# A fused Mamba-2 and MoE-LoRA layer on one core: places of the first products, the base weight sums, the convolution's Silu and the accumulator loads

## The chip, the cores and the metric

The kernel runs on one core of one Trainium2 chip. The metric is the device time of one execution in microseconds (us): from the first to the last work of the program on the core. All data are fp32.

The core's engines run beside one another, each its own instructions in a fixed order: TensorE (PE in the profile) multiplies matrices, VectorE (DVE) and ScalarE (ACT) work on elements, GpSimd (POOL) works on elements too, and SyncE (SP) issues the transfers between DRAM and the on-chip memories. An instruction that is not ready holds up everything behind it on its engine.

## The reference, cut to what matters

One layer over a sequence of 2048 positions with 1024 channels. Two branches share one layer norm:

```python
xn = layernorm(x)                                   # x: (1, 2048, 1024)
# branch 1: Mamba-2 block
gate, hbc, dt = split(xn @ in_proj_w.T)             # 4096, 4096 + 2*1024, 64 channels
xBC  = silu(conv_bias + 4-tap causal conv(hbc))     # per channel
xs, B, C = split(xBC)                               # 64 heads x 64; 8 groups x 128; 8 x 128
dt   = softplus(dt + dt_bias);  dA = exp(dt * A);  A = -exp(A_log)
state = state * dA + (dt * xs) outer B              # for each position, 64 heads
y    = state . C + D * xs
y    = rms_norm(y, groups of 512) * norm_weight * silu(gate)
mamba = y @ out_proj_w.T                            # 4096 -> 1024
# branch 2: linear layer with a mixture of LoRA experts
w    = softmax(top2(xn @ W_router.T))               # 8 experts
ffn  = xn @ W_base.T + b_base + 2 * sum_e w_e * ((xn @ A_e.T) @ B_e.T)   # rank 16
out  = x + mamba + ffn
```

The recurrence is computed by chunks of 128 positions: inside a chunk as a masked product of matrices, from chunk to chunk by a state that each head carries along.

## The kernel before, in words

**Tiles.** The sequence is taken in two parts (`s`, 1024 positions each). A part has two halves of 512, and a half has four chunks of 128. A "block" in the main loop is one group of eight heads in one half of one part: 32 blocks, numbered `b` from 0, four chunks each.

**Projections.** All large products use a recursive scheme with seven products of half-size matrices in place of eight. In the input projections and in the base layer a *pair* of weight tiles (two times 128 output channels) is one such unit: `pair` (from L450) runs seven products for it, and each is four matmuls of 128x128 by 512 positions. Its operands on the weight side come from `left_operands` (from L413): the quarters `a11`, `a12`, `a22` and the sums `s1` to `s4`. With `fresh` set, the sums are made by GpSimd from the quarters and stored to DRAM, to be loaded when the same weights come again; without it they are loaded from there (`kept`). Results leave PSUM through `stored` (from L517): an addition on VectorE or a copy on ScalarE into a tile `ev` (four buffers), for the gate also a Silu on ScalarE, then a store to DRAM. The very first pair is made of four plain products (`plain_pair`, from L497), since its operands arrive piece by piece; a plain product's result is scaled by the layer norm's reciprocal deviation when it leaves PSUM.

`in_pairs` (from L551) gives the order of the pairs. For each part it goes through the eight groups, with three pairs for x, B and C and two for the gate each; then come the base layer's four pairs for part 1, and for part 0. A pair's operands are requested one pair ahead (`ahead`). `stream` is the running list of all products.

**The start.** The layer norm of part 0 is computed in four pieces of 256 positions (`ln_first`, from L194). Each piece passes through steps: mean (`ps_mean`), subtraction and squares, variance (`ps_var`, then Sqrt on ScalarE and a reciprocal on VectorE), scaling. `small_first` (from L884) multiplies the scaled channels by the narrow weights (step sizes, router, LoRA) for two chunks per call, into `ps_sm`. L894 to L912 write out the order of these steps and of the first pair's products on TensorE. `small` (from L297) turns the results into step sizes (softplus), decays (`at`, and `ex` by an Exp on ScalarE, L330), running decays and router weights. For part 1 this is done within blocks 2 to 13, by pieces 0 to 3.

**The convolution.** `load_raw` (L608) brings a block's raw channels, and `conv` (from L624) works on them in steps, one per tile of 128 channels: the first tap by ScalarE (Identity, L635), three more taps by VectorE (L641), and after every second tile a Silu on ScalarE (L647). The main loop runs these steps for the next block during chunks 1 and 2 of the present one, four steps each.

**The scan.** `scan_a` (from L673) prepares a chunk one chunk ahead, in three steps: the scan of decays `es` on VectorE (L682); the product `ps_cb` and its masked form, with `bt` on ScalarE (L694); and the transposition `ps_xt` on TensorE, after which ScalarE writes `xdt` in eight instructions, one per head, each a copy scaled by that head's step size (L707). GpSimd makes `xdd` from it (L83). `scan_b` (from L720) then runs the chunk's products: `ps_y` needs `xdt`, `ps_e` needs the state, `ps_st` needs `xdd` and updates the state. After a block, `norm_squares` and `norm_mean` (L797, `ps_nv`) give the group norm; `ps_nv`, `ps_xt` and `ps_cb` use the same PSUM bank in turn (`aux`).

**Sums for the output weights.** `out_sums` (from L829) makes the first-level sums of `out_proj_w` in 16 units `wo_0` to `wo_15`, one per block from block 15 on: four loads in chunk 0 into a tile with one buffer (tag `wo`, pool opened at block 14), GpSimd additions and stores in chunks 1 to 3.

**Output stage.** From L1045 on: four passes (`t`) of seven units (`u`), each with seven products (`w2` weight tiles, seven buffers, loaded in order ahead of use, L1052). Operands are quarters of y (`load_quarter`, L1076) and their differences on VectorE (`level_one`, `level_two` with tiles `t2`). Results are added into four accumulators, which start as quarters of x (`load_acc`, L1149) and receive the base layer and the LoRA product in `finish_acc` (L1159). Work beside the products is put into `side`, a list of steps for each of the unit's seven products.

**What sets the order.** A planner places each instruction on its engine by estimated times, except those that are pinned with `keep_in_program_order`: these keep the order of the program among themselves and against their neighbours on the engine. All TensorE work is pinned, and GpSimd's work for part 1 (`gp`, L81). Before the change neither the Silu of L647 nor the `xdt` of L707 is pinned. SP's transfers stand in one queue in the order in which they are issued; a store in it waits for the instruction that writes its tile, and a load for its buffer.

## Time and profile before

Three runs took 3481.16, 3479.97 and 3479.03 us; the median is 3479.97. One more execution was profiled, and all rows are from it.

| | |
|---|---|
| median of three runs | 3479.97 us (3479.03 to 3481.16) |
| the profiled execution's own time | 3474.15 us |
| its span | 3471.9 us, at a mean granted clock of 0.995 |
| TensorE without work | 57.5 us of the span |
| DMA | 762.44 MB, mean 220 GB/s |
| HBM | 509.30 MB read, 250.61 MB written |

How to read it: times are in us from the start of the span unless they are called ns. PE is TensorE's matmuls and PEld its weight loads, which overlap them; DVE is VectorE, ACT ScalarE, POOL GpSimd, SP SyncE. A row `PE ps_y L79 <- ACT xdt L707: 9.7, 6, 3.1` says that matmuls into `ps_y`, recorded at line 79, waited for ScalarE's writing of `xdt` at line 707: 9.7 us in all, 6 times, 3.1 at the longest. Line 79 is the helper through which all matmuls go, line 83 the one for GpSimd, so the tile's name tells them apart. In a row of a timeline the first number is the start, the second the length of the group, then engine, line, operation, what is written and read, the shape, the count, and in brackets the wait just before with what ended it. A row of a window gives start:end, its length, the busy time and number of instructions of PE, PEld, VectorE, ScalarE and GpSimd, the granted TensorE clock (1.00 is full speed), DMA's mean busy share and GB/s.

### The profile page before, as it was taken

The numbers are of one execution on the slowest core, as the hardware profiler recorded it, in microseconds if no ns is written. First come the engines' busy times: TensorE is split into PE (matmuls) and PEld (weight loads), VectorE is DVE, ScalarE is ACT, GpSimd is POOL, SyncE is SP. The second block draws the span as 40 slices with busy tenths as digits, with TensorE's granted clock in tenths as the row PEclk, the third lists the DMA queues.
The fourth block names the chain that finished last, engine by engine and source line by source line (L and its number), as shares of the span: only waits on it lengthen the run. The fifth ranks groups of instructions, "written<-read, shape, count | busy, mean of one in ns | idle before, by whom it ended". The sixth has DMA issues, their size and how long they took to land. (4 is left out here: it accounts for less than half of the span.)

```text
span 3471.9 us, 37572 instructions
## 1 busy us (share of the span) xinstructions
PE 3414.4 (98%) x12818; PEld 1995.3 (57%) x12818; DVE 2531.1 (73%) x2861; ACT 933.1 (27%) x2160; POOL 845.3 (24%) x571
## 2 busy tenths in 40 slices
PE   8999999999999999999999999999999999999999
PEld 7444544554554544454445454544444588888888
DVE  6647887887887976687878778878775466666665
ACT  2213343333343333333333233333322000000000
POOL 3233333233333211232233332333442000000000
PEclk9999999999999999999999999999999999999999
DMA  6545565666666687677778878778767777685654
GB/s 222 185 165 198 195 201 186 198 199 198 204 203 200 200 277 219 192 250 238 242 238 256 249 238 247 240 247 239 242 202 259 249 251 243 203 295 191 212 164 146
DMA packets 526286, 762.44 MB, mean 220 GB/s; under 512 B 34704, under 2 KB 264208, under 8 KB 523408
## 3 DMA queue, kind: packets, MB, share of 16 engines
q1 hardware_dynamic: 526096, 760.05, 68.0%
q8 instruction: 102, 1.67, 0.2%
q14 instruction: 88, 0.72, 0.1%
HBM read 509.30 MB, written 250.61 MB: 219 GB/s over the span
## 5 line engine op out<-in xcount | busy, mean ns | idle before, releaser
L682 DVE TENSOR_TENSOR_SCAN es<-dab,here 128x1024 f32<-128x1024 f32 x128 | 323.2, 2525 | 307.9 <-POOL xdd L83 301.3
L83 POOL TENSOR_TENSOR xdd<-xdt,es 128x512 f32<-128x512 f32 x128 | 142.4, 1113 | 989.5 <-ACT xdt L707 926.1
L641 DVE SCALAR_TENSOR_TENSOR xg<-rawx,cw,xg 128x512 f32<-128x512 f32 x384 | 337.7, 929 | 23.5 <-ACT xg L635 23.0
L79 PE MATMUL ps_x_w<-t,w 128*128 128x256 f32 x1344 | 303.8, 379 | 0.0
L707 ACT ACTIVATE xdt<-ps_xt,dt 128x64 f32<-128x64 f32 x1024 | 224.8, 331 | 210.7 <-PE ps_xt L88 210.5
L79 PEld LDWEIGHTS ps_x_w<-t,w 128*128 128x128 f32 x1344 | 255.4, 190 | 41.5 <-issue 7.7
L83 POOL TENSOR_TENSOR state<-state,tot 128x512 f32<-128x512 f32 x112 | 147.1, 1313 | 299.7 <-PE ps_e L79 283.7
L83 POOL TENSOR_TENSOR wo<-wo 128x512 f32<-128x512 f32 (+1 forms) x112 | 216.4, 1932 | 6.3
L79 PE MATMUL ps_a_w<-q,w 128*128 128x256 f32 x896 | 205.1, 382 | 4.0 <-DMA w<-w 4.0
L696 DVE TENSOR_TENSOR dab<-es,cbm 128x1024 f32<-128x1024 f32 x128 | 181.3, 1416 | 17.7 <-ACT cbm L692 17.6
L1297 ACT COPY s<-ps_a_w 128x512 f32<-128x512 f32 x28 | 16.4, 585 | 642.9 <-PE ps_a_w L79 575.6
L79 PEld LDWEIGHTS ps_a_w<-q,w 128*128 128x128 f32 x896 | 171.9, 192 | 28.6 <-issue 4.8
L79 PEld LDWEIGHTS ps_y<-dab,xdt 128*64 128x64 f32 x2048 | 113.8, 137 | 106.1 <-issue 73.4
L79 PE MATMUL ps_x_x<-op_again,s_x 128*128 128x512 f32 x384 | 172.7, 592 | 0.0
L79 PE MATMUL ps_y_x<-op_again,s_x 128*128 128x512 f32 x384 | 172.7, 592 | 0.0
L79 PE MATMUL ps_a_x<-op_again,a_x 128*128 128x512 f32 x384 | 172.7, 592 | 0.0
L79 PE MATMUL ps_x_x<-op,s_x 128*128 128x512 f32 x368 | 165.5, 592 | 0.0
L79 PE MATMUL ps_y_x<-op,s_x 128*128 128x512 f32 x368 | 165.5, 592 | 0.0
L79 PE MATMUL ps_a_x<-op,a_x 128*128 128x512 f32 x368 | 165.4, 592 | 0.0
L641 DVE SCALAR_TENSOR_TENSOR bc<-rawb,cw,bc 128x512 f32<-128x512 f32 x192 | 153.4, 831 | 3.3 <-ACT bc L635 2.6
L79 PE MATMUL ps_y<-dab,xdt 128*64 128x128 f32 x2048 | 145.5, 281 | 9.7 <-ACT xdt L707 9.7
L427 POOL TENSOR_TENSOR s_x<-a_x,a_x 128x512 f32<-128x512 f32 x48 | 78.9, 1643 | 270.1 <-PE ps_y_g L79 65.7
(238 smaller groups left out, 6127.3 us busy)
## 6 DMA issues: line engine op xcount, KB each, us to landing
w<-w SPq DMA_DIRECT2D x196, 512.0 KB, 3.7
dab<-da_d SPq DMA_DIRECT2D x128, 512.0 KB, 5.1
raw<-ev SPq DMA_DIRECT2D x192, 256.0 KB, 3.2
a_x<-in_w_in_dram SPq DMA_DIRECT2D x168, 256.0 KB, 4.0
w<-wo SPq DMA_DIRECT2D x96, 448.0 KB, 3.3
ecp<-run_d SPq DMA_DIRECT2D x256, 128.0 KB, 4.0
gate<-ev SPq DMA_DIRECT2D x128, 256.0 KB, 3.1
sg<-gate SPq DMA_DIRECT2D x32, 1024.0 KB, 7.5
```

Of the source, the lines that this page charges most:

```text
L79: tc.keep_in_program_order(nc.tensor.matmul(*args, **kw))
L83: ins = nc.gpsimd.tensor_tensor(*args)
L427: nc.gpsimd.tensor_tensor(t[what], t[x], t[y], alu)
L641: nc.vector.scalar_tensor_tensor(dst[:, i, :], raw[:, i, k : k + TB], cw[:, ti, k : k + 1], dst[:, i, :], ALU.mult, ALU.add,)
L682: nc.vector.tensor_tensor_scan(es.rearrange("p h t -> p (h t)"), dab.rearrange("p h t -> p (h t)"), here, 0.0, ALU.mult, ALU.add,)
L696: nc.vector.tensor_tensor(ms, es, cbm.unsqueeze(1).to_broadcast([P, HG, Q]), ALU.mult)
L707: nc.scalar.activation(xdt[:, h, :], x_t[:, h, :], AF.Copy, scale=dt_of[s][:, half * NQ + c, at : at + 1],)
L1297: nc.scalar.copy(s1, pa)
```

## The change

Four parts, independent of one another in the code.

1. *The start.* The second call of `small_first` and one plain product now stand ahead of the variances of pieces 2 and 3; the next plain product comes directly behind them. In `plain_pair` the two results of the second half (`n` = 1) leave PSUM after all four products instead of each behind its own.
2. *The base layer's weight sums.* The pairs of the base layer no longer make their sums when their operands are requested. A new function `base_sums` makes them in block 14, one pair per chunk: four loads at the end of a chunk into the tile with tag `wo`, and after the next chunk's `scan_b` four GpSimd sums and four stores into `kept`. The last pair's sums come at the end of block 15's chunk 0, just before the loads of `wo_0`.
3. *The convolution.* A step of `conv` now ends behind its taps; the Silu of two tiles is issued at the start of the following step, and it is pinned. `xdt` is pinned too.
4. *The output stage.* One quarter (`q_0_11`) and three accumulators (`acc_1_01`, `acc_1_11`, `acc_1_10`), loaded ahead of the loop before, are loaded in side steps of the first pass's units 0 and 1. The results' targets are looked up when a result leaves PSUM, not when the unit is set up; `finish_acc` takes its quarter as one argument.

```diff
     def plain_pair(key, name, quarters, quarter):
         t = left_operands(key, quarters, True, first_w)
         yield
+        late = []
         for n in range(2):
             for m in range(2):
...
-                quarter(m, n, ps.rearrange("p a t -> p (a t)"), rstd_of[n], ALU.mult)
+                late.append((m, n, ps.rearrange("p a t -> p (a t)")))
+                if n == 0:
+                    quarter(*late.pop(), rstd_of[n], ALU.mult)
                 yield
+        for m, n, ps in late:
+            quarter(m, n, ps, rstd_of[n], ALU.mult)
+        yield
...
                     f"b{q}", f"b_{s}_{q}", halves(w_base[2 * q], w_base[2 * q + 1]),
-                    lambda s=s: ops_of["x", s], stored(base_d, 2 * q, s, AF.Copy),
-                    s == NS - 1,
+                    lambda s=s: ops_of["x", s], stored(base_d, 2 * q, s, AF.Copy), False,
...
     def conv(s, g, half):
...
+                yield
                 if i % 2:
                     two = dst[:, i - 1 : i + 1, :]
-                    nc.scalar.activation(two, two, AF.Silu)
-                yield
+                    tc.keep_in_program_order(nc.scalar.activation(two, two, AF.Silu))
+        yield
...
     def scan_a(s, g, half, c):
...
-            nc.scalar.activation(
+            ins = nc.scalar.activation(
                 xdt[:, h, :], x_t[:, h, :], AF.Copy,
                 scale=dt_of[s][:, half * NQ + c, at : at + 1],
             )
+            tc.keep_in_program_order(ins)
...
+    def add(*args):
+        gp(1, *args)
+
+    def level_one_sums(t):
+
+        add(t[:, 5], t[:, 0], t[:, 3], ALU.subtract)
+        add(t[:, 3], t[:, 3], t[:, 2], ALU.add)
+        add(t[:, 4], t[:, 3], t[:, 0], ALU.subtract)
+        add(t[:, 6], t[:, 1], t[:, 4], ALU.subtract)
+
+    def base_sums(pool, i):
+
+        t = pool.tile([P, 7, 4, P], F32, tag="wo", name=f"wb_{i}")
+        q11, q12, q21, q22 = halves(w_base[2 * i], w_base[2 * i + 1])
+        for j, src in enumerate((q11, q12, q22, q21)):
+            nc.sync.dma_start(t[:, j], src)
+        yield
+        level_one_sums(t)
+        for j, what in ((3, "s1"), (4, "s2"), (5, "s3"), (6, "s4")):
+            d = dram.tile([P, KH, P], F32, tag=f"{what}_b{i}", name=f"{what}_b{i}_d")
+            nc.sync.dma_start(d, t[:, j])
+            kept[f"b{i}", what] = d
+        yield
...
     small_first(0)
+    small_first(1)
+    next(stream)
     next(lns[2])
-    small_first(1)
     next(lns[3])
+    next(stream)
     next(stream)
     next(lns[2])
     small_first(2)
-    next(stream)
     next(lns[3])
     small_first(3)
     first_sums()
...
+        if b == 15:
+            base_left = left_sums
         if 0 <= b - 15 < 16:
             left_sums = out_sums(wo, b - 15)
...
             scan_b(*blk, c)
+            if b == 14 and c:
+                next(left_sums)
             if 0 <= b - 15 < 16 and c:
                 next(left_sums)
...
+            if b == 14:
+                left_sums = base_sums(wo, c)
+                next(left_sums)
             if 0 <= b - 15 < 16 and c == 0:
+                if b == 15:
+                    next(base_left)
                 next(left_sums)
...
-    def finish_acc(s, a, n):
+    def finish_acc(s, quarter):
+        a, n = quarter
...
     load_quarter(0, 0, 1)
     load_acc(1, 0, 0)
-    load_quarter(0, 1, 1)
-    for a, n in ((0, 1), (1, 1), (1, 0)):
-        load_acc(1, a, n)
...
+            if t == 0 and u < 2:
+                if u == 0:
+                    at(3, load_quarter, 0, 1, 1)
+                    at(5, load_acc, 1, 0, 1)
+                else:
+                    at(1, load_acc, 1, 1, 1)
+                    at(4, load_acc, 1, 1, 0)
...
-            to_add = [kept_sum] if i == 6 else [
-                acc_of[s, *x]
...
+            targets = {
+                2: ((0, 0),), 5: ((0, 1), (1, 1)), 7: ((1, 1), (1, 0)), 3: ((0, 1),), 4: ((1, 0),)
+            }.get(i, ())
 
             def quarter(m, n, ps, add):
                 cols = slice(n * HT, (n + 1) * HT)
+                to_add = [kept_sum] if i == 6 else [acc_of[s, *x] for x in targets]
```

More of the change, by code (lines that the diff above doesn't have):

```diff
@@ L833, in out_sums @@
         x = pool.tile([P, 7, P], F32, tag="wox", name=f"wox_{i}")
-        def add(*args):
-            gp(1, *args)
         def store(j, src):
@@ L847, in out_sums @@
         yield
-        add(t[:, 5], t[:, 0], t[:, 3], ALU.subtract)
-        add(t[:, 3], t[:, 3], t[:, 2], ALU.add)
-        add(t[:, 4], t[:, 3], t[:, 0], ALU.subtract)
-        add(t[:, 6], t[:, 1], t[:, 4], ALU.subtract)
+        level_one_sums(t)
         store(0, t[:, :, 0])
@@ L1239, in mamba_lora_kernel @@
                 quarter = {0: (0, 0), 1: (0, 1), 4: (1, 1), 6: (1, 0)}[u]
-                fin = finish_acc(s, *quarter)
+                fin = finish_acc(s, quarter)
                 for n in (1, 2, 3, 3, 4, 5, 6, 6):
@@ L1247, in mamba_lora_kernel @@
             to_set = [kept_sum] if i == 1 else []
-            to_add = [kept_sum] if i == 6 else [
-                acc_of[s, *x]
-                for x in {2: ((0, 0),), 5: ((0, 1), (1, 1)), 7: ((1, 1), (1, 0)),
-                          3: ((0, 1),), 4: ((1, 0),)}.get(i, ())
-            ]
+            targets = {
+                2: ((0, 0),), 5: ((0, 1), (1, 1)), 7: ((1, 1), (1, 0)), 3: ((0, 1),), 4: ((1, 0),)
+            }.get(i, ())
             def quarter(m, n, ps, add):
                 cols = slice(n * HT, (n + 1) * HT)
+                to_add = [kept_sum] if i == 6 else [acc_of[s, *x] for x in targets]
                 for out in to_set:
```

## The prediction

> **What bounds the kernel now.** I read the page first: busy shares, then the waits of TensorE, then windows of the granted clock around its longest waits, then timelines of ScalarE and GpSimd beside them.

> ```profile
> span 3471.9 us, 37572 instructions
> PE 3414.4 (98%) x12818; PEld 1995.3 (57%) x12818; DVE 2531.1 (73%) x2861; ACT 933.1 (27%) x2160; POOL 845.3 (24%) x571
> ```

> TensorE is the bound. Its products stay the same, so only its 57.5 us without work, and time at a lower clock, can be won or lost.

> ```profile
> PE ps_y L79 <- ACT xdt L707: 9.7, 6, 3.1
> PE ps_var L79 <- ACT sm L892: 6.7, 1, 6.7
> PE ps_nv L79 <- ACT xdt L707: 5.9, 4, 1.7
> PE ps_st L79 <- POOL xdd L83: 5.9, 2, 3.8
> PE ps_mean L79 <- DMA piece<-in_xT_dram: 4.4, 1, 4.4
> PE ps_a_w L79 <- DMA w<-w: 4.0, 1, 4.0
> PE ps_y_g L79 <- DVE s_g L482: 3.5, 1, 3.5
> PE ps_x_x L79 <- DVE ev L525: 3.3, 4, 1.5
> PE ps_st L79 <- ACT mean L253: 2.6, 1, 2.6
> PE ps_xt L88 <- ACT bt L694: 2.2, 2, 1.7
> ```

> Columns are total us, times, longest. Most waits are a few us, spread over the kernel, and each hangs on one instruction's place in another engine's order.

> ```profile
> 1754.00:1764.00 10.00, 7.30 (x35) 4.24 (x34) 6.67 (x9) 3.75 (x10) 2.85 (x2) 1.00 0.88 273
> 2511.00:2521.00 10.00, 7.90 (x26) 4.00 (x25) 5.79 (x5) 0.81 (x2) 8.47 (x5) 0.83 0.61 204
> 2554.00:2564.00 10.00, 6.23 (x18) 3.15 (x15) 5.04 (x3) 0.79 (x2) 3.27 (x3) 0.66 0.46 150
> 2782.00:2792.00 10.00, 6.04 (x18) 4.62 (x17) 8.83 (x7) 0.00 (x0) 0.00 (x0) 0.69 1.04 404
> ```

> The third number from the end is the granted clock. A wait of 2.70 us (1756) left it at 1.00; waits of 2.10 (2513), 3.77 (2555) and 3.96 us (2784) were followed by 3.4, 6.8 and 6.8 us at half clock, so 1.7, 2.6 and 2.5 us of lost time on top.

> **Part 1, the start.** In the timeline TensorE waits 6.70 us at 40.98 for the variance of piece 2, then runs at half clock. The new order puts the step-size groups of chunks 2 and 3 (2.7 us each) and a plain product (6.9) ahead of both variances (0.86 each), then the second plain product (6.9) and four step-size groups (10.8). From 40.84 that is 31.85 us without a gap, ending at 72.7 against 81.55. Is everything there in time? Piece 3, which the plain product reads, is ready at 45.6 and needed at 46.2. VectorE then has two reciprocals (1.75 each), two scalings (1.23) and an eviction (0.68) between the variances and chunk 4: ready at 61.1, needed at 61.7. So 8.9 us gained; between 0 (an operand a few us late) and 8.9. Later waits up to 200 us hang on chains that TensorE itself starts and shift along; VectorE idles 7.25 us at 69 and 10 at 134, so it can follow.

> **Part 2, base's weight sums.** The 16 GpSimd additions of `s1_b0` to `s4_b3` stood among the `xdd` products from 2473 to 2600; each took 1.3 to 3.3 us and waited for its loads, and `xdd` behind them kept TensorE waiting 2.10 and 3.77 us. Both `xdt` inputs were ready 3 to 7 us before. Gain 5.9, and 1.7 + 2.6 of clock: 10.2.
> They now stand in block 14 (1361 to 1463), four per step, 1.6 to 1.8 us each by the next row:

> ```profile
> 1442.19 1.06 POOL L83 TENSOR_TENSOR xdd<-xdt,es 128x512 f32<-128x512 f32 x1 [12.77 <-ACT xdt L707]
> 1446.86 6.92 POOL L83 TENSOR_TENSOR wo<-wo 128x512 f32<-128x512 f32 x4
> 1460.14 1.06 POOL L83 TENSOR_TENSOR xdd<-xdt,es 128x512 f32<-128x512 f32 x1 [6.36 <-DVE xg L641]
> ```

> GpSimd has 12 us of idle per step there, so three of the four groups fit. SP, in order, stands for 6 to 7 us at each group's four stores (they wait for the additions) and again until the last store has landed (2.5 us) before the next loads into the one buffer. Behind it are a decay load (`dab`, used 10 us or more later), `ecp` (20 us or more), projection weights (45), and four evictions' stores (the buffer is reused 25 us later): no price. But the last group ends at 1448 to 1450, its store lands at 1451 to 1453, and only then the four loads of the first output sums `wo_0` start, which stood 130 us earlier before. They land after 4.0 to 5.5 us (rows of those loads), their additions take 5.3 to 6.9, and `xdd` of the next chunk is now behind them: 1463.4 to 1468.8, where TensorE wants it at 1463.1. Loss 0.3 to 5.6, and 0 to 2.5 of clock. I take 4.3, the middle of both. The 28 extra transfers (about 7 MB of 762) lie beside this.

> **Part 3, Silu a step later.** Waits that a Silu ahead of `xdt` made, because it waited for VectorE's taps, go: 2.70 (1756), 0.74 (1981), 1.20 (2057), 1.19 (2430), 3.08 (2595); with `xdt` late, its eight heads also paced TensorE (1.79 us instead of 1.02, five times 0.77), and 1.1 of clock at 2595. The waits at 468 (1.71, `bt`) and 479 (1.57, `da`) had the same Silus ahead and go too. At 2509 a gate Silu still stands ahead: 0.3 of 0.76. Sum 17.5; between 9 (only the bare waits) and 18.5.
> But pinning `xdt` lets the planner put other work ahead of it:

> ```profile
> 452.38 1.74 ACT L707 ACTIVATE xdt<-ps_xt,dt 128x64 f32<-128x64 f32 x8
> ...
> 460.46 0.61 ACT L527 ACTIVATE ev<-ev 128x512 f32<-128x512 f32 x1
> ...
> 463.91 1.28 ACT L330 ACT_TABLE_LOAD   x1
> 467.10 0.31 ACT L330 ACTIVATE ex<-at 128x128 f32<-128x128 f32 x1 [1.91 <-DVE at L329]
> ```

> In the built order the Silu of 460.46, the table load and the Exp of 467.10 all precede this `xdt`. `at` comes earlier now (VectorE's chain runs without the 2.28 us scan and the taps): ready at about 462.5, and table load done at 462.4. So `xdt` ends at 464.5 instead of 454.1, and TensorE, which wants it at 454.3, loses 9.4 us, 12.7 if the small operations keep their long forms (1.0 to 1.3 us). The clock adds 1.7 to 3.4; I take 2.5: 11.9.
> The same Exp for pieces 1 to 3 stands ahead of `xdt` at 708, 954 and 1201: it ends at 712.5, 958.2 and 1205.5, eight heads follow, and TensorE loses 2.6, 1.1 and 2.6 us. Clock 0 to 5.1; I take 1.0, since 1.7 us of bare wait left it at 1.00 elsewhere: 7.3.
> At 1570, 2168, 2317 and 2470 a gate Silu stood between the fifth and sixth head; it is now ahead of all eight, so five heads (5 times 0.2) follow it: the `ps_nv` waits grow by 1.05 each, 4.2, to between 2.1 and 2.8. Clock 0 to 6.8; I take 2.5, since of waits of this size two (2.10, 2.55 at 643) fell to half and one (2.70) did not: 6.7.
> Two `xdd` (728, 1221) go behind two weight additions: 0 to 0.6 each, I take 0.4 in all.

> [...]

> **Part 4, loads of the output stage.** At 2784 TensorE waits 3.96 us for `w2_0_2_1`, issued at 2775.90 behind `q_0_11` and six accumulator loads. It is now issued at 2761.4, landing at about 2774; the next ones keep their lead. VectorE's two subtractions that need `q_0_11` go later, and `t2_0_2_5`, first used at 2790.6 then, is ready at 2789. Gain 3.96 and 2.5 of clock: 6.5; between 3 and 6.5.

> **Sum.** Won: 8.9 + 10.2 + 17.5 + 6.5 = 43.1. Lost: 4.3 + 11.9 + 7.3 + 6.7 + 0.4 = 30.6. Net 12.5 less than the profiled execution's 3474.15 (its span and 2.25 around it). That execution is 5.8 below the median of the runs, so I take the difference from the median: 3479.97 - 12.5 = 3467.5.

> **Rivals.**
> *Half the gain is missing (0.25).* The start hangs on 0.5 us of slack in VectorE and the output stage on 1.6; if the one gives nothing and `at` takes its long price (3.3), net is 0.3: 3479.7. For it: the small slacks. Against: each chain was summed from rows.
> *Slower (0.15): the clock.* Nine waits are made or grown. If each is followed by a full 6.8 us at half clock (3.4 lost), they cost 30.6 instead of the 7.2 in my sum, net +10.9: 3490.9. It decides from 2.2 us a wait on. For it: 2555 and 2784. Against: only waits above 3.7 us had 6.8.
> *The new orders cost little (0.10).* If Exp and gate Silu come early enough (VectorE ahead because TensorE waits), of the losses only 454 at 9.4 and 0.3 of the others stay: net -33, 3447. Against: their inputs need VectorE's chain in any case.
> *It does not do what it says:* for parts 1 and 4 excluded by the built order; for part 3 in four of ten places, which is in the sum.

> **How the numbers follow.** Within 0.2% (7 us) a measurement can't tell it from no change. The forecast (net -20 to -7) has 0.5. Faster: 0.5 and 0.1; same: 0.25; slower: 0.15. Range: low end 3453, most of the losses at their lower bounds (10.5 + 6.3 + 4.2 + 0.3) and the gains kept, then a little beyond; high end 3487, gains at 31 and losses at 38. The forecast's own range is 3460 to 3473.

> **What would show it.** The `ps_var` wait gone; `xdd` waits at 2500 to 2600 gone, one of some 4 us at 1463 in their place; `ps_y <- xdt` now led by one of 9 us near 445, with three of 1 to 2 us; `ps_nv` waits above 2; no wait for `w` near 2775. It would be wrong if the 9 us did not appear, if VectorE kept the start waiting, or if the loads behind SP's stand in block 14 were late.

## The result and the profile after

The changed kernel takes 3459.95 us (median of six runs, 3457.56 to 3462.72), the kernel before 3478.64 us on the same chips (six runs, 3475.63 to 3481.16). The ratio is 0.9946, with a 95% interval of 0.9933 to 0.9959: 18.7 us, or 0.54%, faster. The forecast was 3467.5 us in a range of 3453 to 3487.

The profiled execution of the changed kernel took 3459.94 us. Two lines of its page:

```profile
span 3458.2 us, 37638 instructions
PE 3409.4 (99%) x12818; PEld 1993.4 (58%) x12818; DVE 2530.2 (73%) x2861; ACT 926.4 (27%) x2158; POOL 832.3 (24%) x571
```

The span is 13.7 us shorter than the 3471.9 before. Of this, 8.7 us are time in which TensorE had no work (57.5 before, 48.8 now). The other 5.0 us are in its busy time (3414.4 before, 3409.4 now): the same 12818 matmuls, fewer of them at a granted clock of one half ("half clock": 34.1 us ahead of the last matmul before, 23.9 now).

TensorE's waits by what ended them (total us, times, longest):

```profile
PE ps_y L79 <- ACT xdt L713: 13.4, 5, 6.8
PE ps_nv L79 <- ACT xdt L713: 10.0, 4, 2.7
PE ps_st L79 <- POOL xdd L83: 5.4, 1, 5.4
PE ps_mean L79 <- DMA piece<-in_xT_dram: 4.5, 1, 4.5
PE ps_y_g L79 <- DVE s_g L482: 3.0, 1, 3.0
PE ps_x_g L79 <- DVE ev L531: 2.7, 4, 1.3
...
PE ps_st L79 <- ACT mean L253: 0.6, 1, 0.6
```

The 6.7 us wait for `ps_var` and the 4.0 us wait for `w` are gone. The total behind `xdt` has grown from 15.6 (9.7 and 5.9) to 23.4 us, and its longest wait from 3.1 to 6.8 us. Windows of the changed kernel at its longest waits show the clock in the third number from the end:

```profile
445.00:455.00 10.00, 3.31 (x21) 2.98 (x22) 7.20 (x24) 5.78 (x14) 1.06 (x1) 0.69 0.99 335
1202.00:1212.00 10.00, 7.89 (x34) 5.11 (x33) 6.99 (x13) 4.90 (x14) 2.54 (x2) 0.83 0.90 299
1467.00:1477.00 10.00, 4.62 (x12) 2.34 (x12) 3.97 (x3) 0.00 (x0) 9.77 (x7) 0.83 0.50 145
2478.00:2488.00 10.00, 7.31 (x37) 4.02 (x37) 7.13 (x5) 4.75 (x12) 2.10 (x2) 1.00 0.72 245
```

At 445 only a third of 10 us is work and the clock is at half for 6.8 us. At 1467 GpSimd is busy for 9.77 of 10 us while TensorE does 4.62. At 2478 a wait of 2.69 us left the clock at 1.00.

To see what each place is worth, take the same matmul in both traces and subtract its start after from its start before. This is the changed kernel's lead. Its steps, place by place (times of before, each read between two stretches in which the lead stands still):

| place | lead gained or lost, us | forecast |
|---|---|---|
| start, to 160 | +9.5 | +8.9 |
| 445 to 456, Exp ahead of `xdt` | -8.6 | -11.9 |
| 468 and 479 | +3.5 | +3.3 |
| 553 and 643 | +4.6 | none |
| 702, 953, 1204, Exp ahead of `xdt` | -9.4 | -7.3 |
| 800, a result's buffer | -1.6 | none |
| 1463, base sums in block 14 | -7.2 | -4.3 |
| four norms, 1570 to 2470 | -7.3 | -6.7 |
| 1756, 1981, 2057, 2430, 2509 | +9.1 | +9.2 |
| 2513 and 2555, base sums | +10.6 | +10.2 |
| 2595 | +5.0 | +5.0 |
| 2784, output stage | +6.7 | +6.5 |

The table sums to 14.9; steps under 0.8 us between these places bring the lead to 13.8 at the last matmul.

On ScalarE both kinds of loss look as the forecast described them. The first is the Exp ahead of `xdt`, here at 449 and at 1200:

```profile
449.19 0.63 ACT L533 ACTIVATE ev<-ev 128x512 f32<-128x512 f32 x1 [6.17 <-DVE ev L531]
449.83 1.28 ACT L330 ACT_TABLE_LOAD   x1
451.13 0.31 ACT L330 ACTIVATE ex<-at 128x128 f32<-128x128 f32 x1
451.35 1.73 ACT L713 ACTIVATE xdt<-ps_xt,dt 128x64 f32<-128x64 f32 x8
...
1200.74 1.28 ACT L330 ACT_TABLE_LOAD   x1
1205.46 0.31 ACT L330 ACTIVATE ex<-at 128x128 f32<-128x128 f32 x1 [3.43 <-DVE at L329]
1205.67 1.73 ACT L713 ACTIVATE xdt<-ps_xt,dt 128x64 f32<-128x64 f32 x8
```

At 449 ScalarE stands 6.17 us for a gate result and then has a table load and the Exp to do before the eight heads of `xdt`, whose input `ps_xt` TensorE finished at 441.5. At 1205 it stands 3.43 us for `at`.

The second is the gate's Silu at the norms, here at 1570, before and in the changed kernel:

```profile
1566.96 1.13 ACT L707 ACTIVATE xdt<-ps_xt,dt 128x64 f32<-128x64 f32 x5 [2.75 <-PE ps_xt L88]
1570.72 0.63 ACT L527 ACTIVATE ev<-ev 128x512 f32<-128x512 f32 x1 [2.62 <-issue]
1571.25 0.70 ACT L707 ACTIVATE xdt<-ps_xt,dt 128x64 f32<-128x64 f32 x3
```

```profile
1582.32 0.63 ACT L533 ACTIVATE ev<-ev 128x512 f32<-128x512 f32 x1 [6.51 <-issue]
1582.85 1.72 ACT L713 ACTIVATE xdt<-ps_xt,dt 128x64 f32<-128x64 f32 x8
```

Five heads of `xdt` ran ahead of the Silu before; now all eight stand behind it, and the wait for the last of them is 2.73 us where it was 1.71.

### The profile page after: what moved, and what is told of

Its sections match the earlier page's. It is cut to its first block, busy times and chain, and to the rows that moved or that the text cites. A ratio compares the mean times of both kernels' runs of the same rounds, so it can differ in the third digit from the quotient of the medians.

```text
span 3458.2 us, 37638 instructions
## 1 busy us (share of the span) xinstructions
PE 3409.4 (99%) x12818; PEld 1993.4 (58%) x12818; DVE 2530.2 (73%) x2861; ACT 926.4 (27%) x2158; POOL 832.3 (24%) x571
## 4 chain that ended last, share of the span: by engine, by line
PE 77%; DVE 10%; issue 6%; DMA 4%; POOL 2%; ACT 1%; SPq 0%; POOLq 0%; DVEq 0%; ACTq 0%
PE ps_x_x L79 10%; PE ps_x_w L79 8%; PE ps_a_x L79 7%; PE ps_y_x L79 7%; PE ps_x_g L79 6%; PE ps_a_w L79 6%; PE ps_y_w L79 6%; PE ps_y_g L79 4%; PE ps_a_g L79 4%; PE ps_y L79 3%; PE ps_e L79 3%; PE ps_x_b L79 2%; PE ps_st L79 2%; PE ps_a_b L79 2%; PE ps_y_b L79 2%
## 5 line engine op out<-in xcount | busy, mean ns | idle before, releaser
L83 POOL TENSOR_TENSOR xdd<-xdt,es 128x512 f32<-128x512 f32 x128 | 145.3, 1135 | 1003.4 <-ACT xdt L713 967.6
L79 PE MATMUL ps_x_w<-t,w 128*128 128x256 f32 x1344 | 303.8, 379 | 0.0
L79 PEld LDWEIGHTS ps_x_w<-t,w 128*128 128x128 f32 x1344 | 255.4, 190 | 41.5 <-issue 7.7
L83 POOL TENSOR_TENSOR wo<-wo 128x512 f32<-128x512 f32 (+1 forms) x112 | 214.1, 1912 | 16.6 <-DMA ecp<-run_d 10.3
L83 POOL TENSOR_TENSOR state<-state,tot 128x512 f32<-128x512 f32 x112 | 134.5, 1201 | 322.4 <-PE ps_e L79 311.0
L79 PE MATMUL ps_a_w<-q,w 128*128 128x256 f32 x896 | 202.5, 379 | 0.0
L702 DVE TENSOR_TENSOR dab<-es,cbm 128x1024 f32<-128x1024 f32 x128 | 174.1, 1360 | 27.5 <-ACT cbm L698 27.4
L79 PEld LDWEIGHTS ps_a_w<-q,w 128*128 128x128 f32 x896 | 170.2, 190 | 23.6 <-issue 0.5
L79 PEld LDWEIGHTS ps_y<-dab,xdt 128*64 128x64 f32 x2048 | 114.0, 138 | 109.6 <-issue 72.6
L79 PE MATMUL ps_y_x<-op_again,s_x 128*128 128x512 f32 x384 | 173.3, 594 | 0.0
L79 PE MATMUL ps_x_x<-op_again,s_x 128*128 128x512 f32 x384 | 172.7, 592 | 0.0
L79 PE MATMUL ps_a_x<-op_again,a_x 128*128 128x512 f32 x384 | 172.7, 592 | 0.0
L79 PE MATMUL ps_x_x<-op,s_x 128*128 128x512 f32 x368 | 165.5, 592 | 0.0
L79 PE MATMUL ps_y_x<-op,s_x 128*128 128x512 f32 x368 | 165.5, 592 | 0.0
L79 PE MATMUL ps_a_x<-op,a_x 128*128 128x512 f32 x368 | 165.4, 592 | 0.0
L79 PE MATMUL ps_y<-dab,xdt 128*64 128x128 f32 x2048 | 145.9, 283 | 13.4 <-ACT xdt L713 13.4
L79 PE MATMUL ps_e<-bc,state 128*128 128x128 f32 x960 | 142.1, 292 | 0.0
```

The costliest lines, as they stand in the source:

```text
L79: tc.keep_in_program_order(nc.tensor.matmul(*args, **kw))
L83: ins = nc.gpsimd.tensor_tensor(*args)
L702: nc.vector.tensor_tensor(ms, es, cbm.unsqueeze(1).to_broadcast([P, HG, Q]), ALU.mult)
```

## The experiments

The theory: the four parts act at different places; the later Silu, the start, the base sums' removal from the end and the output loads gain; the pin of `xdt` and the place of the last base sum lose. Rivals are named with each run. Every run is compared with runs of the kernel before on its own chip; where a gain is given in us beside a ratio, it is worked out from that ratio.

### Each part alone

**The start alone.** The kernel before with:

```diff
     small_first(0)
+    small_first(1)
+    next(stream)
     next(lns[2])
-    small_first(1)
     next(lns[3])
+    next(stream)
     next(stream)
...
-    next(stream)
```

and the late results of `plain_pair`.

> The kernel before with part 1 (order of the start) alone. Theory (the parts add up): the 6.70 us wait for `ps_var` and its 3.4 us of lost clock go, two small ones grow; TensorE runs about 9 us earlier from 60 us on and keeps this to the end: span some 9 us shorter than the kernel before, ratio about 0.9974, all later waits unchanged within 1 us. Rival (absorbed): a later operand is the true limit, the lead is gone by 500 us and the ratio is 1.000. Rival (it makes the wait near 445): the earlier start alone turns the order at 445 to 455 into a wait of several us; then the ratio is above 0.998 and the page shows that wait.

Measured: ratio 0.9975 (0.9964 to 0.9986), 8.7 us faster; no wait near 445. TensorE leads the kernel before by 8.7 us at 100 and 7.0 at 160 (the wait for `s_g` at 142 is 3.81 here, 3.48 before), and still by 7.3 at 1750. Both rivals fall. In this one profile only 2.4 us of the lead are left at the end: a half clock behind 1749 takes 1.2, and waits behind loads that this part does not touch are longer here (6.15 us at 2548, 3.76 at 2589, 5.10 at 2780, where before had 3.77, 3.08 and 3.96). The ratio, from eight runs, stands against that.

**Base's sums alone.** The kernel before with `base_sums`, its calls in blocks 14 and 15, and:

```diff
-                    lambda s=s: ops_of["x", s], stored(base_d, 2 * q, s, AF.Copy),
-                    s == NS - 1,
+                    lambda s=s: ops_of["x", s], stored(base_d, 2 * q, s, AF.Copy), False,
```

> The kernel before with part 2 (base's weight sums in block 14) alone. Theory: the two `xdd` waits at 2513 and 2555 with their half clock go (2.10 + 3.77 + 1.7 + 2.6, together 10 to 11 us) and one `xdd` wait of 5 to 6 us with 1.7 us of half clock comes near 1463 to 1480: net 3 to 4 us shorter, ratio about 0.999. Rival: the wait after block 14 belongs to the pinned `xdt` of part 3 (a later `xdt` makes `xdd` late), so that it is absent here: net 10 us shorter, ratio 0.997.

Measured: ratio 0.9977 (0.9967 to 0.9987), 8 us faster, where the theory had 3 to 4. The ratio alone would fit the rival's 0.997. The trace decides: the wait after block 14 is there without the pin of `xdt`, at 1460, so the rival falls:

```profile
PE ps_st L79 <- POOL xdd L83: 4.9, 1, 4.9
```

The lead falls by 7.2 us at 1464 and rises by 13.7 between 2507 and 2603, where 10 to 11 had been expected: with the base sums away the wait for `xdt` at 2595 is shorter too (3.08 before, 1.06 here).

**Silu and the two pins alone.** The kernel before with:

```diff
+                yield
                 if i % 2:
                     two = dst[:, i - 1 : i + 1, :]
-                    nc.scalar.activation(two, two, AF.Silu)
-                yield
+                    tc.keep_in_program_order(nc.scalar.activation(two, two, AF.Silu))
+        yield
...
+            tc.keep_in_program_order(ins)
```

> The kernel before with part 3 (Silu a step behind its taps, Silu and `xdt` pinned) alone. Theory: it removes about 17 us of waits behind Silu (468, 479, 1756, 1981, 2057, 2430, 2595) and adds about 25: 8 to 12 near 454, some 10 at 708 to 1205 (the Exp ahead of `xdt`), 6.7 at the four `ps_nv` (gate Silu ahead of all heads). Net 8 us longer, ratio 1.002. Rival: the wait near 445 comes from the earlier start and not from the pin; then this part alone is 0 to 10 us shorter, ratio 0.997 to 1.000.

Measured: ratio 1.003 (1.002 to 1.004): this part alone is slower, by some 11 us. Its waits:

```profile
PE ps_st L79 <- POOL xdd L83: 13.6, 3, 6.5
PE ps_y L79 <- ACT xdt L708: 12.1, 5, 6.6
PE ps_nv L79 <- ACT xdt L708: 10.0, 4, 2.7
```

The 6.6 us wait at 454 is there without the earlier start, so it belongs to this part. The first line was not expected: 13.6 us for `xdd`, 5.9 before. GpSimd in this kernel, from 2566 on:

```profile
2566.03 1.26 POOL L427 TENSOR_TENSOR s_b<-a_b,s_b 128x512 f32<-128x512 f32 x1 [5.29 <-DMA a_b<-in_w_base_dram]
2567.25 1.06 POOL L83 TENSOR_TENSOR xdd<-xdt,es 128x512 f32<-128x512 f32 x1
...
2609.52 1.26 POOL L427 TENSOR_TENSOR s_b<-a_b,s_b 128x512 f32<-128x512 f32 x1 [8.06 <-DMA a_b<-in_w_base_dram]
2610.74 1.06 POOL L83 TENSOR_TENSOR xdd<-xdt,es 128x512 f32<-128x512 f32 x1
```

Base's additions stand ahead of `xdd` and wait for their loads, 5.29 and 8.06 us. So at 2595 the Silu's gain is taken back at once by `xdd` (5.78 us at 2606). From 2508 to 2611 this part alone loses 3.9 us and part 2 alone wins 13.7, together 9.8; in the changed kernel the same stretch wins 15.9. Some of these 6 us are the one profile of before, whose loads came early: the start alone and the output loads alone, with this stretch as before, lose 1.8 and 2.3 us in it. That explains about 2; the other 4 are an interplay of the two parts. Two causes held up the same chunk, `xdt` by 3.08 us and the additions ahead of `xdd` by 5.78, and the removal of the first is worth something only when the second is gone too.

**The output loads alone.** The kernel before with:

```diff
-    load_quarter(0, 1, 1)
-    for a, n in ((0, 1), (1, 1), (1, 0)):
-        load_acc(1, a, n)
...
+            if t == 0 and u < 2:
+                if u == 0:
+                    at(3, load_quarter, 0, 1, 1)
+                    at(5, load_acc, 1, 0, 1)
+                else:
+                    at(1, load_acc, 1, 1, 1)
+                    at(4, load_acc, 1, 1, 0)
```

> The kernel before with part 4 (accumulator loads between products) alone. Theory: the 3.96 us wait for `w2` at 2784 and 2.5 to 3.4 us of half clock behind it go, nothing else moves: 6.5 to 7 us shorter, ratio 0.998. Rival: the quarter or an accumulator loaded later is late for its first use; then a wait on VectorE's differences or on a result's target appears between 2790 and 2860 and the gain is under 3 us.

Measured: ratio 0.9982 (0.9973 to 0.9991), 6.3 us faster. The wait for `w` is gone (4.0 before) with the half clock behind it, and nothing of 0.6 us or more follows after 2600. The rival falls.

Together the four ratios make 0.9964, against 0.9946 for the whole change; each interval is 0.001 each way, so the ratios alone don't tell these apart. The plain medians of the same runs are 5.2, 6.7 and 5.2 us below the kernel before and 11.7 above it, 5.4 us in all, so the times don't say how well the parts add up. The traces show one place where they do not, 2508 to 2611.

### What the pin of `xdt` costs, and what the later Silu brings

**The changed kernel without the pin of `xdt`:**

```diff
-            ins = nc.scalar.activation(
+            nc.scalar.activation(
                 xdt[:, h, :], x_t[:, h, :], AF.Copy,
...
-            tc.keep_in_program_order(ins)
```

> The changed kernel with `xdt` unpinned; the Silu stays a step later and pinned. Theory (the later Silu is the gain, the pin of `xdt` the loss): the planner puts `xdt` ahead of the four Exp and of the gate Silu again, the waits at 445, 702, 953 and 1204 go with their half clock (12.9 + 5 us) and the four `ps_nv` waits shrink from 10.0 to some 6 in all, while the waits behind the convolution's Silu stay away: span 22 to 25 us below the changed kernel's 3458.2, about 3434, ratio to the kernel before about 0.988. Rival (the pin is what keeps `xdt` ahead of the Silu): waits of 1 to 3 us at 1756, 1981, 2057, 2430 come back and the span is 3445 or more.

Measured: ratio 0.9905 (0.9888 to 0.9921), span 3439.5, 18.7 us below the changed kernel. Its waits for `xdt`, and ScalarE near 445:

```profile
PE ps_nv L79 <- ACT xdt L713: 5.9, 4, 1.7
...
PE ps_y L79 <- ACT xdt L713: 1.9, 1, 1.9
```

```profile
442.11 1.74 ACT L713 ACTIVATE xdt<-ps_xt,dt 128x64 f32<-128x64 f32 x8
449.42 0.63 ACT L533 ACTIVATE ev<-ev 128x512 f32<-128x512 f32 x1 [5.57 <-DVE ev L531]
449.96 2.92 ACT L640 ACTIVATE xg<-rawx,cb,cw 128x512 f32<-128x512 f32 x4
452.89 1.28 ACT L330 ACT_TABLE_LOAD   x1
455.92 0.31 ACT L330 ACTIVATE ex<-at 128x128 f32<-128x128 f32 x1 [1.74 <-DVE at L329]
```

`xdt` runs at 442, ahead of the Silu and the Exp, and no wait behind a convolution's Silu has come back: in this kernel the pin of `xdt` only costs. The gain is 3 to 6 us below the 22 to 25 expected, for two reasons in the trace. One wait for `xdt` (1.95 us at 947, with 1.7 of half clock) is left, since the planner put only five of its heads ahead of the Exp. And of the 8.7 us won at 445, 4.6 are given back by 551, most of them to waits that had lain behind the longer one: `bt` 0.95, `s_g` 0.70, a result's buffer 1.50.

**The changed kernel with the Exp a step later, both pins kept:**

```diff
+        yield
         nc.scalar.activation(ex, at, AF.Exp)
...
-            if after == 1 and c in (0, 2, 3):
+            if after == 1:
                 side += steps(rest, 1)
```

(and one more `next(later)` at the start).

> The changed kernel with the Exp of part 1's pieces issued a step later, behind the next `xdt`; both pins stay. Theory: the waits for `xdt` at 445 (6.76), 702 (1.33), 953 (2.74) and 1204 (2.11) and their lost clock (3.4 + 1.7) go, the `ps_nv` waits stay at 10.0: span 16 to 19 us below 3458.2, about 3441, ratio about 0.990. Rival (the wait is VectorE's, whose chain up to `at` delays whatever comes next, so that `es` or the transposition of `ex` becomes late): waits of some us on `xdd` or `ps_da` take their place and the span stays above 3450.

Measured: ratio 0.992 (0.9905 to 0.9935), span 3445.9, 12.3 us below the changed kernel. Its waits:

```profile
PE ps_nv L79 <- ACT xdt L714: 10.0, 4, 2.7
...
PE ps_y L79 <- ACT xdt L714: 0.5, 1, 0.5
```

13.4 us of waits before `ps_y` have become 0.5, and `ps_nv` is untouched, so moving the Exp alone removes these waits. At 445 `xdt` now also runs ahead of the gate's Silu, which had stood before the Exp:

```profile
444.64 1.74 ACT L714 ACTIVATE xdt<-ps_xt,dt 128x64 f32<-128x64 f32 x8
452.52 0.63 ACT L534 ACTIVATE ev<-ev 128x512 f32<-128x512 f32 x1 [6.14 <-DVE ev L532]
```

The same waits as above (1.72, 0.70, 1.53) gave back most of 5 us by 551, as the rival had it for other waits. The span, 3445.9, lies between the 3441 of the theory and the 3450 of the rival.

**The changed kernel with the Silu back in its old step**, unpinned, `xdt` still pinned:

```diff
-                yield
                 if i % 2:
                     two = dst[:, i - 1 : i + 1, :]
-                    tc.keep_in_program_order(nc.scalar.activation(two, two, AF.Silu))
-        yield
+                    nc.scalar.activation(two, two, AF.Silu)
+                yield
```

> The changed kernel with the convolution's Silu back in its old step and unpinned; `xdt` stays pinned. Theory (the later Silu is the whole gain of part 3): the Silu stands ahead of `xdt` again and waits there for VectorE's taps, so waits for `xdt` of 1 to 3 us come back behind it, as at 1756, 1981, 2057 and 2430 before, and with them what follows from them: 10 to 17 us above 3458.2, span 3468 to 3475, ratio about 0.998; the waits at 445, 702, 953 and 1204 stay. Rival (the pin of `xdt` already keeps the Silu behind it): span within 3 us of 3458.2.

Measured: ratio 0.9975 (0.9965 to 0.9984), by the ratios some 10 us above the changed kernel, the low end of what was expected. The profiled span, 3462.8, and the median, 3466.72 (a span of some 3465), lie below the expected 3468 to 3475, but above the rival's 3 us. The trace shows the loss and what hides part of it. TensorE leads the changed kernel by 7.2 us at 1590 and is 4.1 behind it at 2593: 11 us lost on the way. The lead ahead of that was not expected: of the waits that should have stayed, those at 702 and 1204 are only 0.72 and 1.22 us here, and the one at 953 is gone (the Exp starts 3.3 us earlier, since VectorE has `at` ready earlier); why that is so, no run shows. ScalarE at 1765:

```profile
1765.19 1.06 ACT L652 ACTIVATE xg<-xg 128x1024 f32<-128x1024 f32 x1 [2.38 <-DVE xg L646]
1766.15 1.73 ACT L712 ACTIVATE xdt<-ps_xt,dt 128x64 f32<-128x64 f32 x8
```

The Silu stands ahead of `xdt` and waits 2.38 us for the taps; TensorE waits 3.03 us. The waits at 1988, 2064 and 2439 are back too (0.74, 1.70, 1.18), and at 636 that for `mean` (2.56). The rival falls: the pin of `xdt` keeps no Silu away. Whether the later step or the Silu's own pin does it, no run separates.

### The two other losses, and all together

**The last base sum earlier:**

```diff
+            if b == 15 and c == 0:
+                next(base_left)
             if 0 <= b - 15 < 16 and c:
                 next(left_sums)
...
-                if b == 15:
-                    next(base_left)
                 next(left_sums)
```

> The changed kernel with the last of base's weight sums in block 15 directly behind the scan of chunk 0, as in the other chunks, and not at that chunk's end. Theory: the loads of `wo_0` then start 10 us or more earlier, and the 5.38 us wait for `xdd` at 1467 with 1.7 us of half clock goes: span about 3451, ratio about 0.9925. Rival: the additions of `wb_3` now wait for their own loads and hold the `xdd` of the next chunk instead: a wait of similar size near 1446, span 3456 to 3460.

Measured: ratio 0.9923 (0.9908 to 0.9938), span 3444.8. GpSimd in the changed kernel, and then in this one:

```profile
1446.60 1.06 POOL L83 TENSOR_TENSOR xdd<-xdt,es 128x512 f32<-128x512 f32 x1 [12.77 <-DMA y<-xg]
1447.62 7.74 POOL L83 TENSOR_TENSOR wb<-wb 128x512 f32<-128x512 f32 x4
...
1466.69 5.29 POOL L83 TENSOR_TENSOR wo<-wo 128x512 f32<-128x512 f32 x4 [10.34 <-DMA ecp<-run_d]
1471.94 1.06 POOL L83 TENSOR_TENSOR xdd<-xdt,es 128x512 f32<-128x512 f32 x1
```

```profile
1427.52 5.31 POOL L83 TENSOR_TENSOR wb<-wb 128x512 f32<-128x512 f32 x4
1440.33 1.06 POOL L83 TENSOR_TENSOR xdd<-xdt,es 128x512 f32<-128x512 f32 x1 [7.50 <-ACT xdt L713]
...
1445.00 6.14 POOL L83 TENSOR_TENSOR wo<-wo 128x512 f32<-128x512 f32 x4
1459.10 1.14 POOL L83 TENSOR_TENSOR xdd<-xdt,es 128x512 f32<-128x512 f32 x1 [7.95 <-ACT xdt L713]
```

In the changed kernel the sums of `wb_3` run at 1448 to 1455, the loads into the same tile are issued from 1457.58 on, the last of them lands at 1466.48, and the sums of `wo_0` start at 1466.69, with `xdd` behind them. (The brackets name other transfers; the releaser is inferred.) With the base sum earlier, `wo_0` is summed by 1451 and GpSimd waits for `xdt`, not the reverse. TensorE wins 7.2 us on the changed kernel here, as expected (5.38 and 1.7), and no wait appears near 1446, so the rival falls. The other 6 us of the span lie ahead of it, 2.1 before 160, 2.5 at 1204 and the rest in smaller steps, where the code is the same and the waits and the clock differ between executions.

**The norm's product behind `ps_y`:**

```diff
+    def scan_b(s, g, half, c, between=None):
...
             mm(psy[o, j, :], xdt[:, h, :], ms[:, h, :], start=True, stop=True)
+        if between:
+            norm_mean(*between)
...
-            if c == 0 and prev:
-                norm_mean(*prev)
-            scan_b(*blk, c)
+            scan_b(*blk, c, prev if c == 0 else None)
```

(the tile `y` is taken behind the norm's product, not ahead of it).

> The changed kernel with the norm's product `ps_nv` behind `ps_y` of the same chunk instead of ahead of it. `ps_nv` has to wait for all eight heads of `xdt`, `ps_y` only for the first. Theory: the four waits (2.73, 2.10, 2.44, 2.69) shrink by what seven heads take (7 times 0.2) and `ps_y` runs beside the remaining heads: 1.5 to 1.8 us each, 6 to 7 in all, and up to 3.4 of clock: span 3448 to 3452, ratio about 0.992. Rival: `ps_nv` comes 2 us later, and the norm's chain on ScalarE and VectorE behind it then keeps another product waiting: span unchanged within 2 us.

Measured: ratio 0.9915 (0.99 to 0.993), span 3446.2. The four waits for `xdt` are now 1.31, 0.67, 1.01 and 1.26 us and stand before `ps_y`, no half clock follows them, and TensorE wins 6.6 us on the changed kernel at the four places, as the theory had it. The rest of the span's 12 us lies mainly at 800 (1.6) and 1204 (3.2).

**All three edits together**, and then **with `xdt` unpinned as well** (the diffs above):

> The changed kernel with the three single edits of before together: Exp a step later, the last of base's sums directly behind the scan, `ps_nv` behind `ps_y`. Theory (three separate places): the gains measured at those places add up, 12.3 at 445 to 1210, 7.3 at 1467 and 6.3 at the four norms: 26 us below 3458.2, span about 3432, ratio about 0.9875; the longest wait after 200 us is under 2 us. Rival: what is gained at one place is waited for at another, as the waits for `bt` and `ev` near 460 and 545 took back some 4 us after 445; then the span is 3437 or more.

> As the three edits together, and `xdt` unpinned as well. Theory: the planner puts the gate's Silu between the heads, so that the waits for `xdt` that are left at the four norms (about 1.3, 0.7, 1.0, 1.3) shrink to 0.3 or less: 4 us below the three edits alone, span about 3428, ratio about 0.9865. Rival: unpinned heads with a gate Silu among them pace TensorE at seven other places where they were in time; then no difference, or 1 to 3 us longer.

Measured: ratio 0.9865 (0.9849 to 0.9882), median 3428.77 us, and 0.9858 (0.9843 to 0.9873), median 3425.76 us. Each beats the kernel before by about 1.4%, and the changed kernel by 0.8 to 0.9%. Between them the intervals and the spans (3425.1 and 3427.3) don't decide: unpinning saved 3.3 us at the four norms, where 4 had been expected, but this execution had lost 5.7 before 500 us: 4.4 ahead of 160, where the code is the same (the wait at 141 is 2.61 in the one and 3.29, with half clock, in the other), and the rest at 494, in a new wait of 1.61 for `xdd`. The three edits:

```profile
span 3425.1 us, 37674 instructions
...
PE ps_y L79 <- ACT xdt L714: 4.7, 5, 1.3
PE ps_mean L79 <- DMA piece<-in_xT_dram: 4.3, 1, 4.3
PE ps_y_g L79 <- DVE s_g L483: 2.6, 1, 2.6
...
PE ps_st L79 <- POOL xdd L83: 0.2, 1, 0.2
```

The gains at the three places add up: 16.2 at 445 to 1210, 7.2 at 1467 and 7.4 from 1570 on (6.6 of them at the norms), with 2.5 from the start; 33 us in the span where 26 were expected. Part of the surplus is steps at 800 and between 970 and 1195, which other runs show too and none of the three edits was meant for. After 200 us no wait is longer than 1.52 us, and the clock does not drop within the span. What was given back near 460 and 545 (1.51, 0.70, 1.29) is the part of the rival that holds.

## Why the prediction was right, point by point

The forecast's net was 12.5 us; the two profiles differ by 13.8 at the last matmul, the medians by 18.7. The time lies in the range and the mechanisms are the ones named, but the closeness of 12.5 and 13.8 is in part luck. Gains that the sum lacked, 4.6 us at 553 and 643 and 1.4 more at the places it named, nearly cancel losses that it lacked, 1.6 at 800, 1.2 in small steps and some 2 more at the places it named. The distance from 13.8 to 18.7 the sum does not explain.

*The start (8.9).* Right: at 100 us the lead is 8.5 in the changed kernel and 8.7 alone. The chain with 0.5 us of slack held. Waits up to 160 that differ between executions make it 9.5 and 7.0.

*Base's sums (10.2).* Right: 10.6. (At 2555 the sum took 2.6 us for the clock; the drop is 6.83 us long and 1.85 of it lie within the wait, which leaves 2.5.) But in the profile of before the two waits for `xdd` were 2.10 and 3.77 us, 5.9 together; the three further kernels with base's sums in the same place had 7.6, 7.8 and 8.3. They hang on when loads land, and the one profile that the sum was made from shows a mild case. That may be part of why the profiled executions differ by 14.2 us and the medians by 18.7; it was not shown on the runs behind the medians.

*The loss in block 14 (4.3).* Right mechanism, mis-sized: a wait of 5.38 us, at the upper end of the 0.3 to 5.6 given, and 1.6 of clock, with small steps 7.2 in all. The base additions took 7.74 us where four of 1.6 to 1.8 had been taken, and the loads of `wo_0` took 5.6 to 6.8 us to land where 4.0 to 5.5 had been taken.

*Silu's waits (17.5).* 17.7 at the places named, with two errors in them. The wait for `bt` at 468 was not the Silu's: with the Silu late and the Exp moved it is back (1.72 us). In the changed kernel it is hidden because TensorE comes late from 445, and so is the wait at 553 (back with 1.53). And the Silus also stood ahead of `mean`: the wait `ps_st <- ACT mean` at 643, 2.55 us, is 0.61 now and 2.56 with the Silu in its old step. It stood in the list of waits, and the sum followed only those that name `xdt`, `bt` and `da`.

*Exp ahead of `xdt` at 454 (11.9).* Right mechanism, too dear: a wait of 6.76 us and 8.6 in all. The term that was mis-sized is the time at which the Exp can start: `at` was ready at 450.7 and the table load done at 451.1, where the forecast's 462.5 and 462.4, less its 8.9 us of lead, make 453.6 and 453.5. The clock cost 2.0, not 2.5, since 2.9 of the 6.8 us at half clock lie within the wait.

*Exp at 708, 954, 1201 (7.3).* 9.4. The waits are 1.33, 2.74 and 2.11 where 2.6, 1.1 and 2.6 were forecast, so the second was off most; the clock dropped at the last alone (0.83 in the window at 1202, 1.7 us lost where 1.0 was taken). The remaining 1.5 us are `ps_y` running at the pace of the heads behind each late `xdt`, which the sum had for other places but not here.

*The norms (6.7).* Right: waits of 2.73, 2.10, 2.44 and 2.69 us, in the 2.1 to 2.8 given; two of the four had half clock behind them, 3.2 us where 2.5 had been taken, which makes 7.3 in all.

*Output loads (6.5).* Right: 6.7, and 6.7 in the profile of this part alone.

*The rivals.* Slower by the clock: nine waits were made or grown, as counted, and five of them were followed by half clock (445 by 6.8 us, four by 3.4). As 2.9 us of the first and 0.3 of the one at 1467 lie within the wait, that is 8.6 us lost, where the sum had 7.2 and the rival 30.6. "The new orders cost little" was wrong in the changed kernel, where the losses it speaks of are 32.5 us by the table; the runs without the pin and with the Exp later show what it would have been worth, 18.7 and 12.3 us. That the gain would be half missing was wrong too: start and output stage brought their full terms.

## What to carry to other kernels

Pinning an instruction binds it to everything that stands ahead of it in the program, not only to the neighbour that the pin was meant for; print the built order around each pinned instruction and look for work of other chains (here an Exp and a gate's Silu) that has come ahead of it. When two causes hold up the same product, remove one alone and the other takes its place: price them together. And when a work buffer with one copy passes from one use to the next, place the last use by when the next one's loads must start.

## What the runs showed of the hardware

How long the waits were that cost clock as well. In the thirteen profiles (before, after and eleven experiments) waits of TensorE from 0.95 to 1.8 us were followed by half clock in none of 88 cases, those of 1.8 to 3.0 us in 25 of 41 (the shortest 1.95 us), those of 3.0 to 4.2 us in 13 of 16, and longer ones in all 21. Drops last 3.4 or 6.8 us (3.413 or 6.827 in the kernel before and in the changed one; over 4.2 us of wait 18 of 21 had the longer one) at a granted clock of 0.50, so they cost 1.7 or 3.4 us at most; what of a drop lies within the wait costs nothing more, as 2.9 of the 6.8 us at 445.

A profile of one execution can mislead on single waits. The wait for `s_g` at 141 hangs on a load of the convolution's channels and was 2.3 to 3.8 us long from one kernel with the new start to the next. The one at 1204 hangs on `at`, at the end of a long chain on VectorE: it was 2.11 us in the changed kernel and 0.73 with the last base sum earlier, an edit that lies some 240 us behind it; what made the chain later, no run shows. The four waits for `xdt` before `ps_nv`, which hang on the order of ScalarE's instructions (1.71, 1.08, 1.42, 1.66), came back to 0.02 us in five profiles.
